# Cross-attention with token branch: another order for setup and the first two batches

## The chip, the cores and the metric

The kernel runs on one core of one Trainium2 chip. A core has five instruction queues that run beside each other: TensorE (PE, matrix products into PSUM; its weight loads are shown apart as PEld), VectorE (DVE), ScalarE (ACT), GpSimd (POOL, "Pool" below) and SyncE (SP), which here only issues DMA transfers. Each queue works in its own order; an instruction that waits holds up everything behind it on its queue. The metric is the device time of one execution in microseconds; the median of several executions is compared.

## What is computed

Sixteen batches of 100 queries and a context of 722 rows, of which the last four are "tokens". The parts that matter:

```python
query = hidden_states @ Wq;  keyt = enc @ Wk;  valt = enc @ Wv      # enc: 718 context rows x 384
hs = _mha(query, keyt, valt)                                        # 8 heads of 80
ca_q1 = jnp.einsum('btc,th->bch', ca, Wq_ca)[:, indices, :]         # ca: 4 tokens x 384
ca_hs1 = _mha(ca_q1, residual, residual)
ca_q2 = ca_hs1 @ Wq;  ca_k2 = ca @ Wk_ca;  ca_v2 = ca @ Wv_ca
ca_hs2 = _mha(ca_q2, ca_k2, ca_v2)
out = (hs + ca_hs2) @ Wout + b_out + residual
```

All of it is in 32-bit floats.

## The kernel before

**Context products with fewer multiplications.** The 718 context rows are cut into three thirds (240 columns each, u = 0, 1, 2), the 384 channels into three chunks, the 640 outputs into halves or pairs. From batch 1 on, a product of a batch's context with Wv (class `Values`, line 395) or Wk (class `Keys`, line 438) is made from 15 products of *forms* instead of 18: sums of the context's pieces times sums of the weights' pieces, listed in `V_PLAN` and `K_PLAN` with the PSUM bank, the form and the place that each feeds. The context's forms are made by `enc_sums` (line 466, 13 tensor_tensor of 128 x 240 on Pool for each batch; form 7 is the seventh written), the weights' forms once by `weight_sums` (line 487): seven early sums, which write fresh places, and five late ones, which overwrite raw weights, so everything that reads the raw weights must be done before them. Batch 0 uses raw pieces: `first_values` (line 353) and `first_keys` (line 561). The fifth block of 128 outputs of the keys is always made raw, by `last_keys` (line 568), whose two ScalarE copies into kT are line 554.

**Token branch.** Class `Second` does it per batch: `products` (y_ps and g), `scores1` (seven Pool instructions that form e from the tokens `ca` and g; lines 756 and 763), `softmax1` (its maximum by transposes on VectorE, lines 650 to 680, then line 773), `exponentials1`, `softmax2` (z_ps and z), `scores2` (lines 810 to 822), `softmax3` (lines 828 to 831), `load` (the tokens' values vb from DRAM, issued by Pool, line 802) and `values2` (seven Pool instructions into hs2, lines 845 and 852). `keys` (line 691) masks the small matrices m for a batch on Pool.

**One batch of the main loop** (from line 1089): `scores` (s_ps on PE, ScalarE copies to st, VectorE takes the row maximum `most`), `softmax2`, `products` of the next batch, `Maximum` of `most`, then the values of this batch and the keys of the next interleaved (`vv.go`, `kk.go`), `subtract` (line 1111) and `exponential` (line 1119) of three st tiles, `last_keys` of the next batch, now and then `project` (o_ps, which needs 128 finished rows; batches 0, 10 and 14 have none there), queries for the next two batches in odd batches, then the attention products a_ps (line 1272), which read st. hs, the result, has hs2 added (line 1294 in batch 0, line 1292 later) and is transposed by PE in the next batch (`Last.transpose`, line 891). Everything from line 1088 on is issued in the order in which it is written; above that a scheduler orders it, except the loads marked `in_order`.

**Setup.** SP loads the context of batch 0 (`load_first`), the tokens, Wq transposed (wqt, into wout_sb), x transposed (xT), Wk transposed in a packed order (wkt, into kT, five loads), Wq (five loads) and Wv of the tokens. PE makes the first values (v_ps), the token matrices (k_ps, m_ps, y_ps), turns wkt (w_ps, line 1028; copies alternately on ScalarE and VectorE, line 1031), then the first keys, va_ps and the queries. VectorE rearranges Wq into wq_sb (lines 1039 and 1046).

Buffers that matter: `rest` (one buffer, two context pieces of a batch), `enc` (two), `ca` (two), `hsT` (two), `vb` (one). The order in batches 0 and 1 around the change:

```python
if b == 0:                      # line 1128
    now.load()
    now.softmax1()
    for late in (False, True):
        weight_sums(nc.vector, wk_sb, late)
    enc_sums(enc)
    weight_sums(nc.gpsimd, wv_sb, False)
...
if b == 1:                      # line 1141, between the row maxima of tiles 1 and 2
    weight_sums(nc.vector, wv_sb, True)
```

Of the kernel before, what the change touches and what calls it, by code (L numbers as in the profile page):

```python
# [8 lines left out]
F32 = mybir.dt.float32  # L9
# [5 lines left out]
B, S, H = 16, 100, 640  # L15
NH, D = 8, 80
CAD, T = 384, 4
# [3 lines left out]
CC = CAD // P  # L21

KT = SK // 3 + 1
# [101 lines left out]
def kernel(  # L125
# [84 lines left out]
    def rest_tile(name):  # L210
        return main.tile([P, len(A_REST), KT], F32, tag="rest", name=name)
# [9 lines left out]
        return enc  # L221

    def load_rest(b, enc):
        rest = rest_tile(f"rest_{b}")
        for (u, c), i in A_REST.items():
            nc.sync.dma_start(
                out=rest[:, i], in_=enct[b][:, c, u * (KT - 1) : u * (KT - 1) + KT]
            )
        return enc[0], rest
# [9 lines left out]
    def in_order(dma):  # L239
        tc.keep_in_program_order(dma)  # L240
# [15 lines left out]
    def load_first(lo, hi, u, cols):  # L256

        for c in range(lo, hi):
            k = u * (KT - 1)
            in_order(  # L260
                nc.sync.dma_start(
                    out=a_raw(enc, u, c)[:, cols],
                    in_=enct[0][:, c, k + cols.start : k + cols.stop],
                )
            )
# [6 lines left out]
                in_=wv[c * P : (c + 1) * P, g * (H // 2) : (g + 1) * (H // 2)],  # L272
            )
    load_first(0, CC, 1, slice(KN, KT))
    for u in (2, 0):
        load_first(0, CC, u, slice(0, KT))
    tokens = vb_tile("tokens")
    cat_sb = tokens[:, CC, : CC * B * T].rearrange("p (c n) -> p c n", c=CC)
    wkca_sb = tokens[:, :CC, :]
# [2 lines left out]
    wqt_sb = wout_sb  # L282
    wkt_sb = kT.rearrange("p c u k -> p c (u k)")
    in_order(nc.sync.dma_start(out=wqt_sb, in_=wqt.rearrange("(c p) r -> p c r", p=P)))
    xT = inp.tile([P, 2, HC, S], F32, tag="xT", name="xT_0")
    in_order(nc.sync.dma_start(out=xT, in_=xt[0:2].rearrange("b p c s -> p b c s")))
    for c in range(HC):
        in_order(nc.sync.dma_start(out=wkt_sb[:, c, :CAD], in_=packed(wkt, c)))  # L288
    halves = [t[:, u] for t in [scores_tile(f"wq_{i}") for i in range(NP)] for u in range(2)]
# [83 lines left out]
    class Blocks:  # L373


        def __init__(self, plan):
            self.opened, self.begun = {}, set()
            self.plan = iter(enumerate(plan))
            self.ends = {bank: k for k, (bank, _, _) in enumerate(plan)}
# [181 lines left out]
    def first_keys(enc):  # L561
        for n in range(HC - 1):
            banks = [psum(f"kT_ps_0_{n}_{k}") for k in range(2)]
            weights = [wk_sb[:, 2 * c + n % 2, n // 2] for c in range(CC)]
            chunk_keys(n, banks, weights, enc)
        last_keys(0, enc)
# [136 lines left out]
    class Second:  # L703


        def __init__(self, b, xT):
            self.b, self.xT = b, xT[:, b % 2]
            self.top = None

            self.ca = small.tile([S, T, S], F32, tag="ca", name=f"ca_{b}", bufs=2)  # L710
            nc.sync.dma_start(
                out=self.ca, in_=cas[b].unsqueeze(0).to_broadcast([S, T, S])
            )
# [288 lines left out]
    for c in range(HC):  # L1002
# [12 lines left out]
            m_ps.rearrange("p (h b t) -> p h b t", h=NH, b=B),  # L1015
        )
        nc.sync.dma_start(out=m_d[c], in_=m_sb[c])
    second = Second(0, xT)
    keys(load_m(0))
    summed = second.products()  # L1020
    second.copy()
# [3 lines left out]
    for c in range(HC):  # L1025
        w_ps = psum(f"w_ps_{c}")
        for cc in range(CC):
            nc.tensor.transpose(
                w_ps[:, cc * P : (cc + 1) * P], wkt_sb[:, c, cc * P : (cc + 1) * P], ident
            )  # L1030
        (dve if c % 2 else act)(
            wk_sb[:, c % 2 : 6 : 2, c // 2] if c < HC - 1 else wk4,
            w_ps[:, : CC * P].rearrange("p (a n) -> p a n", a=CC),
        )

    with tc.issue_after(summed.ins):
        for c in range(HC):
            for u in range(2):
                nc.vector.tensor_copy(
                    wq_sb[:, c, 2 * u * P : 2 * (u + 1) * P].rearrange(  # L1040
                        "p (a r k) -> p a r k", a=2, r=RG
                    ),
                    wq_in[c].rearrange("p (r k) -> p r k", r=RG)[:, :, u * D : u * D + 64]
                    .rearrange("p r (a k) -> p a r k", a=2),
                )
            nc.vector.tensor_copy(
                wq_sb[:, c, 4 * P :].rearrange("p (h k) -> p h k", h=NH),
                wq_in[c].rearrange("p (h k) -> p h k", h=NH)[:, :, 64:],
            )
    first_keys(enc)  # L1050

    va = wide("va")[:, : H // 2]
    va_ps = psum("va_ps")
# [35 lines left out]
    for b in range(B):  # L1089
# [5 lines left out]
        def loads():  # L1095

            if b == 0:
                nc.sync.dma_start(
                    out=wout_sb, in_=wout.rearrange("(c p) n -> p c n", p=P)
                )  # L1100
            if b + 2 >= B:
                return None, None, None
            x_next = xT_at[0] if b % 2 else load_x(p + 1)
            xT_at[0] = x_next
            return Second(b + 2, x_next), load_enc(b + 2), load_m(b + 2)
# [12 lines left out]
        def exponential(i):  # L1118
            nc.scalar.activation(st[i], st[i], AF.Exp, scale=SCALE)  # L1119
# [6 lines left out]
            return most_now  # L1126

        if b == 0:
            now.load()
            now.softmax1()  # L1130
            for late in (False, True):
                weight_sums(nc.vector, wk_sb, late)
            enc_sums(enc)
            weight_sums(nc.gpsimd, wv_sb, False)
        st.append(scores(b, 0, tiles))
        if b == 0:
            now.exponentials1()
        nc.vector.tensor_tensor(most[:KN], st[0][:, 0], st[0][:, 1], ALU.max)
        st.append(scores(b, 1, tiles))
        larger(1)  # L1140
        if b == 1:
            weight_sums(nc.vector, wv_sb, True)
        st.append(scores(b, 2, tiles))

        now.softmax2()
# [6 lines left out]
            kk = Keys(b + 1, enc)  # L1152

        if b == 0:
            now.scores2()
            now.softmax3()
            second.scores1()
            top.go(3)
            kk.go(3)
            top.go(1)  # L1160
            first_values(3, e_in, (act, act), (0,), bank)
            kk.go(2)
            top.go()
            first_values(3, e_in, (act, act), (1,), bank)
            kk.go(3)
            first_values(0, e_in, (act, act), (0,), bank)
            kk.go(2)
            subtract(0)
            exponential(0)
            first_values(0, e_in, (act, act), (1,), bank)  # L1170
            kk.go(2)
            subtract(1)
            kk.go(3)
            exponential(1)
            second_next, enc_next, m_next = loads()
            last_keys(b + 1, enc)
            subtract(2)
            exponential(2)
            now.values2()
            second.load()  # L1180
            second.softmax1(4)
        elif b + 1 < B:
            last.transpose()
            vv = Values(b, e_in)

            def both(n):
                vv.go(n)
                kk.go(n)

            second.scores1(seen)  # L1190
            last.load()
            top.go(3)
            both(3)
            now.scores2()
            top.go(1)
            both(2)
            top.go()
            both(2)
            both(1)
            now.softmax3()  # L1200
            now.values2()
            vv.go(2)
            kk.go(1)
            subtract(0)
            exponential(0)
            vv.go(1)
            subtract(1)
            vv.go(1)
            kk.go(2)
            exponential(1)  # L1210
            vv.go(1)
            kk.go(2)
            both(1)
            both(1)
            second.load()
            second_next, enc_next, m_next = loads()
            subtract(2)
            last_keys(b + 1, enc)
            exponential(2)
            if b + 2 < B:  # L1220
                enc_next = load_rest(b + 2, enc_next)
            second.softmax1()
            last.project()
        else:
            room = enc_tile("spare").rearrange("p f k -> p (f k)")
            spare.extend(room[:, i * H : (i + 1) * H] for i in range(2))
            last.transpose()
            vv = Values(b, e_in)
            last.load()
            mine.load()  # L1230
            top.go(3)
            vv.go(3)
            last.project_few(len(OC) - 2)
            now.scores2()
            top.go(1)
            vv.go(2)
            top.go()
            vv.go(3)
            now.softmax3()
            now.values2()  # L1240
            vv.go(2)
            subtract(0)
            exponential(0)
            vv.go(5)
            for i in (1, 2):
                subtract(i)
                exponential(i)
            last.project()
        if b + 2 < B:
            if b == 0:  # L1250
                enc_next = load_rest(b + 2, enc_next)
            keys(m_next)
            enc_sums(enc_next)
        if b % 2 and b + 1 < B:
# [96 lines left out]
```

## Time and profile before

| What | Value |
|---|---|
| Executions shown | 961.81, 962.16, 964.65 us; median 962.16 |
| Profiled execution | 964.32 us, of which the span from first to last instruction is 962.6 us |
| Granted TensorE clock, mean | 0.995 |
| Busy: PE, PEld, DVE, ACT, POOL | 941.2 (98%), 799.9 (83%), 673.1 (70%), 359.1 (37%), 632.9 us (66%) |
| DMA | 62.48 MB, mean 65 GB/s |

The page cuts the span into 40 equal slices of 24 us, each digit being a busy share in tenths (9 is 90% or more):

```profile
PE   8898989999999999999999999999999999999998
DVE  1357796696947869496874959569694786928883
POOL 4269999485955768487673958738695576836613
PEclk9899999999999999999999999999999999999999
DMA  7930304022040301304050040401204031120100
```

PE is below nine tenths only in the first slices (setup and batches 0 and 1) and in the last. The chain that ended last is followed back from the last instruction to what released it:

```profile
PE 93%; DVE 2%; SPq 2%; DMA 2%; ACT 1%; issue 1%; ACTq 0%; DVEq 0%
```

A later batch takes about 56 us (a_ps starts at 165.6 us in batch 1 and at 902.8 us in batch 14); batch 0 begins near 67 us and batch 1 near 111 us of the span (the first scores, s_ps).

### The profile page before, as it was taken

Reading aid. Unit: us, or ns where it says so; the run is one execution under the profiler, and the core shown is the slowest. Engines: PE = TensorE matmul, PEld = TensorE weight load, DVE = VectorE, ACT = ScalarE, POOL = GpSimd, SP = SyncE. Lnnn points to the kernel's source line nnn. Section 1 sums busy time; section 2 is a strip of 40 time slices with the busy share of each in tenths; the row PEclk is TensorE's granted clock in tenths of the full one; section 3 lists DMA queues with packets and bytes.
Section 4 is the critical chain, followed back from the end, with each engine's and each line's share of the span. In section 5 each row is a group of like instructions: output and inputs, shape, how many; then the busy total and the mean of one; then the engine's idle time right before and its main releaser. Section 6 shows DMA issues by size and latency. Waiting matters only on the chain.

```text
span 962.6 us, 25608 instructions
## 1 busy us (share of the span) xinstructions
PE 941.2 (98%) x11215; PEld 799.9 (83%) x11215; DVE 673.1 (70%) x1083; ACT 359.1 (37%) x596; POOL 632.9 (66%) x572
## 2 busy tenths in 40 slices
PE   8898989999999999999999999999999999999998
PEld 6797869888798798978889787897879878898866
DVE  1357796696947869496874959569694786928883
ACT  1124433433424443342434334243432444325351
POOL 4269999485955768487673958738695576836613
PEclk9899999999999999999999999999999999999999
DMA  7930304022040301304050040401204031120100
GB/s 247 280 120 4 99 1 134 3 56 75 1 148 2 92 24 49 89 1 128 1 142 9 1 129 1 134 3 46 70 3 147 2 95 35 49 80 1 59 8 29
DMA packets 45256, 62.48 MB, mean 65 GB/s; under 512 B 13337, under 2 KB 37209, under 8 KB 43545
## 3 DMA queue, kind: packets, MB, share of 16 engines
q1 hardware_dynamic: 41608, 42.97, 15.1%
q0 software_dynamic: 2512, 16.72, 6.1%
q8 instruction: 88, 1.44, 0.6%
q10 hardware_dynamic: 1024, 1.15, 0.3%
q14 instruction: 24, 0.19, 0.1%
HBM read 55.26 MB, written 5.57 MB: 63 GB/s over the span
## 4 chain that ended last, share of the span: by engine, by line
PE 93%; DVE 2%; SPq 2%; DMA 2%; ACT 1%; issue 1%; ACTq 0%; DVEq 0%
PE s_ps L598 12%; PE a_ps L1272 11%; PE v_psA L419 10%; PE v_psB L419 8%; PE kT_ps L543 8%; PE k_psA L450 7%; PE q_ps L519 7%; PE o_ps L923 7%; PE k_psB L450 6%; PE v_psC L419 3%; PE k_psC L450 3%; PE v_psD L419 2%; PE v_psE L419 2%; PE y_ps L721 2%; PE k_psE L450 1%; SPq L288 1%
## 5 line engine op out<-in xcount | busy, mean ns | idle before, releaser
L756 POOL TENSOR_TENSOR e<-ca,g 100x800 f32<-100x800 f32 x64 | 99.3, 1562 | 155.4 <-DVE most L1123 118.7
L845 POOL TENSOR_TENSOR hs<-vb,p 100x640 f32<-100x640 f32 x64 | 105.6, 1660 | 42.5 <-DVE p L831 40.0
L1272 PEld LDWEIGHTS a_ps<-vs,st 120*64 120x64 f32 (+3 forms) x3072 | 109.1, 125 | 10.9 <-ACT st L1119 5.4
L852 POOL TENSOR_TENSOR hs<-hs,hs 100x640 f32<-100x640 f32 x48 | 115.3, 2402 | 3.8
L1272 PE MATMUL a_ps<-vs,st 120*64 120x81 f32 (+3 forms) x3072 | 112.5, 234 | 4.9 <-ACT st L1119 4.9
L419 PE MATMUL v_psA<-wv_sb,enc 128*120 128x320 f32 x360 | 113.2, 437 | 2.6 <-DVE wv_sb L506 2.6
L485 POOL TENSOR_TENSOR enc<-enc 128x240 f32<-128x240 f32 x135 | 103.9, 784 | 7.1
L1111 DVE TENSOR_TENSOR st<-st,over 120x1600 f32<-120x1600 f32 x48 | 108.0, 2253 | 0.0
L598 PE MATMUL s_ps<-qp,kT 32*120 32x100 f32 x3072 | 98.8, 263 | 0.7 <-issue 0.7
L598 PEld LDWEIGHTS s_ps<-qp,kT 32*120 32x120 f32 x3072 | 95.8, 179 | 2.5 <-issue 1.1
L763 POOL TENSOR_TENSOR e<-e,e 100x800 f32<-100x800 f32 x48 | 95.2, 1983 | 3.8
L615 ACT COPY st<-s_ps 120x800 f32<-120x800 f32 x64 | 49.7, 829 | 128.0 <-PE s_ps L598 128.0
L419 PE MATMUL v_psB<-wv_sb,enc 128*120 128x320 f32 x300 | 93.5, 434 | 0.0
L450 PE MATMUL k_psA<-enc,wk_sb 128*128 128x240 f32 x360 | 87.9, 367 | 2.5 <-DVE kT L390 1.4
L1283 DVE RECIPROCAL rs<-a_ps 100x4 f32<-100x4 f32 x32 | 5.8, 181 | 117.3 <-PE a_ps L1272 117.1
L419 PEld LDWEIGHTS v_psA<-wv_sb,enc 128*120 128x120 f32 x360 | 65.0, 184 | 26.0 <-issue 3.7
L450 PEld LDWEIGHTS k_psA<-enc,wk_sb 128*128 128x128 f32 x360 | 68.2, 190 | 19.9 <-DVE kT L390 1.9
L1123 DVE TENSOR_TENSOR most<-most,st 120x800 f32<-120x800 f32 x64 | 65.6, 1025 | 22.3 <-ACT st L609 21.2
L1119 ACT ACTIVATE st<-st 120x1600 f32<-120x1600 f32 x48 | 74.0, 1543 | 11.4 <-DVE st L1111 11.4
L419 PEld LDWEIGHTS v_psB<-wv_sb,enc 128*120 128x120 f32 x300 | 55.2, 184 | 22.5 <-issue 0.7
L450 PE MATMUL k_psB<-enc,wk_sb 128*128 128x240 f32 x300 | 73.0, 366 | 0.0
L485 POOL TENSOR_TENSOR enc<-enc,rest 128x240 f32<-128x240 f32 x45 | 34.7, 772 | 57.9 <-DMA rest<-in_enct 22.7
(138 smaller groups left out, 1762.5 us busy)
## 6 DMA issues: line engine op xcount, KB each, us to landing
vb<-va_d POOLq DMA_DIRECT2D x16, 1000.0 KB, 7.6
enc<-in_enct SPq DMA_DIRECT2D x30, 240.0 KB, 3.7
enc<-in_enct SPq DMA_DIRECT2D x15, 360.0 KB, 3.5
xT<-in_xt SPq DMA_DIRECT2D x8, 500.0 KB, 4.6
rest<-in_enct SPq DMA_DIRECT2D x31, 120.0 KB, 6.5
xn<-in_x SPq DMA_DIRECT2D x11, 320.0 KB, 9.2
out<-xn SPq DMA_DIRECT2D x11, 320.0 KB, 2.4
ca<-in_cas SPq DMA_DIRECT2D x16, 156.2 KB
```

The costliest lines, as they stand in the source:

```text
L419: nc.tensor.matmul(at[0][j][:KN, : H // 2], a_form(self.enc, f)[:, j * KN : (j + 1) * KN], wv_sb[:, W_AT[f]], start=first, stop=last, skip ...
L450: nc.tensor.matmul(at[:, i * KT : (i + 1) * KT], wk_sb[:, W_AT[f], i], a_form(self.enc, f), start=(first and i == 0), stop=last, skip_grou ...
L485: nc.gpsimd.tensor_tensor(out, left, right, op)
L543: nc.tensor.matmul(bank[:, i * KT : (i + 1) * KT], weights[c], a_raw(enc, u, c), start=(i == 0 and c == 0), stop=(c == CC - 1), skip_group ...
L598: nc.tensor.matmul(s_ps[r][:n, 256 * a + lo : 256 * a + hi], kT[rows, c, u, j * KN : (j + 1) * KN], rhs, start=(a == 0 and c == 0), stop=( ...
L756: first = nc.gpsimd.tensor_tensor(to, self.ca[:, t, :].unsqueeze(1).to_broadcast([S, NH, S]), g[:, :, t].unsqueeze(2).to_broadcast([S, NH, ...
L763: nc.gpsimd.tensor_tensor(e, e, to, ALU.add)
L845: first = nc.gpsimd.tensor_tensor(to, vb[:S, t, :].rearrange("p (h d) -> p h d", h=NH), p2[:, :, t].unsqueeze(2).to_broadcast([S, NH, D]), ...
L852: nc.gpsimd.tensor_tensor(sums, sums, to, ALU.add)
L1111: return nc.vector.tensor_tensor(st[i], st[i], top.over[:KN].unsqueeze(1).to_broadcast([KN, 2, ROWS]), ALU.subtract,)
L1119: nc.scalar.activation(st[i], st[i], AF.Exp, scale=SCALE)
L1272: nc.tensor.matmul(a_v[lo:hi, h % 4], st[i // 2][: KEYS[i], i % 2, h * S + lo : h * S + hi], block(i, h // 4)[: KEYS[i], h % 4], start=(i ...
```

## The change

Six things are moved; no instruction of the computation is added or left out; some change their engine.

- Weights' sums: the 12 of wk_sb and the seven early ones of wv_sb run on VectorE right after Wq has been rearranged, before the first softmax; the five late ones of wv_sb run on Pool at the end of batch 0 instead of VectorE in batch 1.
- Context's sums of batch 1 are issued on Pool ahead of the load of vb_0; those of batch 2 come after values2 of batch 0. vb_1 is loaded in batch 1, behind `scores1` of batch 2, instead of at the end of batch 0.
- In batch 0, `scores2` stands after the first keys and the maximum's first steps, `softmax3` after the keys' and values' additions; values2 waits for the last subtraction (`less`).
- In batches 0 to 14 the last exponential stands ahead of `last_keys` and so of its copies.
- Setup's loads: three context pieces go behind wqt; the tokens of batch 0 (`ca_0`) are loaded ahead of wkt; `rest_1` is loaded into a free hsT buffer.
- All five copies of w_ps run on ScalarE.

```diff
     def load_rest(b, enc):
-        rest = rest_tile(f"rest_{b}")
+        if b == 1:
+            room = hsT_tile("rest_1").rearrange("p c s -> p (c s)")
+            rest = room[:, : len(A_REST) * KT].rearrange("p (i k) -> p i k", k=KT)
+        else:
+            rest = rest_tile(f"rest_{b}")
...
-    for u in (2, 0):
-        load_first(0, CC, u, slice(0, KT))
+    load_first(0, CC, 2, slice(0, KT))
...
     in_order(nc.sync.dma_start(out=wqt_sb, in_=wqt.rearrange("(c p) r -> p c r", p=P)))
+    load_first(0, CC, 0, slice(0, KT))
     xT = inp.tile([P, 2, HC, S], F32, tag="xT", name="xT_0")
     in_order(nc.sync.dma_start(out=xT, in_=xt[0:2].rearrange("b p c s -> p b c s")))
+    ca_0 = small.tile([S, T, S], F32, tag="ca", name="ca_0", bufs=2)
+    in_order(nc.sync.dma_start(out=ca_0, in_=cas[0].unsqueeze(0).to_broadcast([S, T, S])))
...
-        (dve if c % 2 else act)(
+        act(
             wk_sb[:, c % 2 : 6 : 2, c // 2] if c < HC - 1 else wk4,
...
+    for w in wk_sb, wv_sb:
+        with tc.issue_after(summed.ins):
+            weight_sums(nc.vector, w, False)
     first_keys(enc)
+    weight_sums(nc.vector, wk_sb, True)
...
         if b == 0:
+            enc_sums(enc)
             now.load()
             now.softmax1()
-            for late in (False, True):
-                weight_sums(nc.vector, wk_sb, late)
-            enc_sums(enc)
-            weight_sums(nc.gpsimd, wv_sb, False)
...
-        if b == 1:
-            weight_sums(nc.vector, wv_sb, True)
...
         if b == 0:
+            second.scores1()
+            kk.go(3)
+            top.go(3)
             now.scores2()
-            now.softmax3()
-            second.scores1()
-            top.go(3)
-            kk.go(3)
             top.go(1)
...
             kk.go(3)
+            now.softmax3()
             first_values(0, e_in, (act, act), (0,), bank)
...
             second_next, enc_next, m_next = loads()
+            less = subtract(2)
+            exponential(2)
             last_keys(b + 1, enc)
-            subtract(2)
-            exponential(2)
-            now.values2()
-            second.load()
+            enc_next = load_rest(b + 2, enc_next)
+            keys(m_next)
+            weight_sums(nc.gpsimd, wv_sb, True)
+            now.values2(less)
+            enc_sums(enc_next)
             second.softmax1(4)
...
             second.scores1(seen)
+            if b == 1:
+                now.load()
             last.load()
...
             subtract(2)
+            exponential(2)
             last_keys(b + 1, enc)
-            exponential(2)
...
-        if b + 2 < B:
-            if b == 0:
-                enc_next = load_rest(b + 2, enc_next)
+        if 0 < b < B - 2:
             keys(m_next)
             enc_sums(enc_next)
```

`Second` takes the loaded `ca_0` as an argument for batch 0 instead of loading it itself.

## The prediction

> **What bounds the kernel now.** I read the share of busy time first: TensorE (PE) is busy 941.2 of 962.6 us and the chain that ended last is 93% PE, so time can be won only where PE stands still or runs at a lower clock. Next comes the list of who waited for whom, for PE alone:
>
> ```profile
> PE a_ps L1272 <- ACT st L1119: 4.9, 3, 1.6
> PE v_psA L419 <- DVE wv_sb L506: 2.6, 1, 2.6
> PE w_ps L1028 <- DMA kT<-in_wkt: 2.4, 1, 2.4
> PE m_ps L1005 <- DMA wout_sb<-in_wqt: 1.8, 1, 1.8
> PE k_psA L450 <- DVE kT L390: 1.4, 1, 1.4
> PE idle_ps L971 <- DVE idle L968: 1.1, 1, 1.1
> PE k_psA L450 <- ACT kT L392: 1.1, 1, 1.1
> PE s_ps L598 <- issue: 0.7, 1, 0.7
> PE kT_ps L543 <- DVE wk_sb L1031: 0.7, 1, 0.7
> ```
>
> Columns: total us, times, longest. All waits but two a_ps ones and the 0.7 of s_ps lie in the first 124 us. The timeline places them: a_ps at 104.79 (batch 0), 675.24 (batch 10) and 905.26 (batch 14), 1.64 us each; v_psA at 123.38 (batch 1); w_ps at 33.80; the k_psA waits at 82.01 and 86.94 (batch 0). The weight-load rows (PEld) of the same stalls read 1.80, 1.60 and 1.95 us; these are better, since ends of matmuls are modelled. Last, the windows around the wv_sb stall:
>
> ```profile
> 120.70:123.40 2.70, 0.07 (x2) 0.05 (x1) 2.67 (x4) 0.00 (x0) 2.62 (x4) 0.93 0.00 0
> 123.40:124.40 1.00, 1.00 (x2) 0.75 (x3) 1.00 (x2) 0.00 (x0) 0.92 (x2) 0.50 0.00 0
> 124.40:125.40 1.00, 1.00 (x3) 0.58 (x2) 0.97 (x3) 0.00 (x0) 1.00 (x2) 0.50 0.00 0
> 125.40:126.40 1.00, 1.00 (x3) 0.58 (x3) 1.00 (x3) 0.59 (x2) 1.00 (x2) 0.50 0.00 0
> 126.40:127.40 1.00, 1.00 (x5) 0.66 (x5) 0.96 (x2) 0.94 (x3) 0.92 (x2) 0.99 0.00 0
> ```
>
> After the length stand PE, PEld, DVE, ACT, POOL, then the granted clock: PE idles 2.7 us and then gets half the clock for 3 us.
>
> PE's own instructions stay the same (two m_ps products trade places), so each part is a question of which stall goes and what is late next.
>
> **Batch 1, weights' sums.** Five wv_sb sums (L506) sit on VectorE between the row maxima; v_psA waits for the third. From the first z_ps (118.40) to the first k_psA (128.18) batch 1 takes 9.78 us; batch 2, with the same order and no sums, takes 185.15 - 179.75 = 5.40. The stall's price is thus 4.38 us: 2.8 idle and some 1.6 of slow clock. [...] The row shows 0.50 after 2.7 us, so I take 4.4.
> The five sums move to Pool, behind the masked products of batch 2 and ahead of values2 of batch 0. Pool's row for this sum is 861 ns x7, so 4.3 us. What Pool then owes PE next is form 7 of batch 2's context for k_psA: the seventh of 13 sums (L485), which stand behind values2 in both orders. Before: values2 104.4 to 115.1, products to 119.0, seventh sum about 125.4, needed at 128.2. After: Pool's e products for batch 1 start when g is there (77.7, was 87.7) and are done by about 91; the mb load is issued when enc_0 is free (before: 96.3, some 2 us sooner now) and lands about 3 us later (longest wait 3.1); products to 100.5, sums to 104.8, values2 (9.7 alone: 4 x 1.27 + 3 x 1.55) to 114.5, seventh sum at 0.78 us a step about 120 to 121.5. PE, some 8 us ahead of before, asks at 120.4. I charge 0.5 us, with 0 and 2.5 as ends (2.5 if values2 is slowed as in its worst row, 2.79 for one product). hs2 at 114.5 holds up L1294 and the maxima behind it on VectorE, but the transposes of hs are not due before 116.5. **Gain 3.9.** If the Pool cover is gone, see rival 1.
>
> **Batch 0, VectorE and ScalarE order.** Three things leave VectorE: the 12 wk_sb sums (66.45 to 72.07), softmax3 ahead of the maximum, and the contention between the sums and Pool's enc_sums. The contention shows as one row: two Pool sums took 5.20 us at 65.74, where a free one takes 0.70. All 19 sums now run from about 39.4, where VectorE was idle 18.18 us until 57.60: by the row of nine in 3.09 us, 12 x 0.343 + 7 x 0.343 x 320/256 = 7.1 us, the last five not before first_keys is through with wk_sb (53.3), so to about 55. Pool's e products run there too, but with ca_0 there they start at about 31 instead of 45.43 and are done by about 44. The cover is that idle; without it 5.6 us would fall on softmax1. Pool's 13 sums then take some 10 us from 64, not 64.96 to 81.92, and seven wv sums (5.8 us) leave Pool.
> ScalarE: L822 no longer stands ahead of the three kT copies (81.28 behind a 3.19 us wait), so the first k_psA stall, 1.6, goes. The second then meets this row of the chain of waits:
>
> ```profile
> 79.98 0.52 DVE s L810
> ...
> 82.00 0.83 DVE p L831
> ...
> 85.88 0.32 DVE mx L662
> 86.22 0.67 DVE kT L390
> 86.94 1.08 PE k_psA L450 x4
> ```
>
> Without s, mx2, e, sm and p ahead (79.98 to 82.83) the transpose starts at 79.5 to 81, 3.45 us of maximum bring 83 to 84.5, scores2 now stands here (1.3), L390 ends at 85.0 to 86.4. PE could come at 83.4 (86.94 less the two stalls), so it waits 1.6 to 3.1 at this place, and the two stalls together shrink from 3.55 by 0.5 to 1.9; I take 1.4, near the better end because the maxima lose Pool's contention (2.54 and 2.38 for pairs whose free row is 0.99 each). VectorE's subtractions start as before (the copy that spreads the maximum ends near 86.4 to 87 and some 4 us of transpose, kT additions and softmax3 follow: 90.9 against 90.78), but run free of Pool's e products (1.82 each, were 1.82, 2.87, 2.03), so the last exponential can end near 101.7; PE comes to a_ps at 100.95 (102.37 less 1.4) and issues 0.65 us of products on the first two tiles. Stall left about 0.3 of 1.8: 1.5. **Gain 2.9**, ends 1.0 and 4.
>
> **Last exponential ahead of the kT copies, every batch.**
>
> ```profile
> 902.95 0.82 ACT L554 COPY kT<-kT_ps 128x480 f32<-128x480 f32 x2 [3.09 <-PE kT_ps L543]
> 903.65 1.55 ACT L1119 ACTIVATE st<-st 120x1600 f32<-120x1600 f32 x1
> ```
>
> ScalarE sat idle 3.09 us for the kT products while st was subtracted by 900.5 (L1111 at 897.99, 2.48 long). Swapped, the exponential ends at about 902.1, before a_ps starts at 902.84; the copies still follow their products, and kT is read only by the next scores. The stall goes in batches 10 and 14, the two with neither queries nor a projection between: 2 x 1.8, **gain 3.5** (ends 3.2 and 3.6). In the other batches (b=2: a_ps at 219.37, exponential done 216.35) nothing waited: nothing.
>
> **Setup.** On SP three enc loads of 120 KB go behind wqt, and ca_0 (156 KB) ahead of wkt. wqt comes about 1 us sooner, but PE then only waits longer at w_ps for wkt (33.77 before). Moved past ca_0, wkt is later. The row: in 22 to 24 us the DMA engines are busy 0.26 to 0.34 at 95 to 122 GB/s, so wkt moves on few engines; 156 KB at the 300 GB/s of the wide loads would be 0.5 us. [...] I take 0.6. The third wkt load must now also wait for wqt, with two of its kind still queued: nothing, up to one chunk's spacing (2.9 us) if they are gone. Against it, w_ps copies all on ScalarE free their banks at once, where VectorE's stood behind the wq copies (36.03): the weight-load wait of 1.06 goes. **Gain 0.5**, ends +1.5 and -2.3.
> The loads of rest_1 (into a free hsT buffer, early), rest_2 (behind mb) and vb_1 (issued by Pool behind the e products of batch 2, near 139, landing 7.6 later at 147, so values2 of batch 1 ends near 160; its first reader, L1292, comes at 161.5) cost nothing; that last cover is thin, but beyond it the hs transposes leave 10 us more.
>
> **Sum.** 3.9 + 2.9 + 3.5 + 0.5 = 10.8 us. The profiled execution took 964.32 (span 962.6 and 1.7 around it), so 953.5; the median of the runs shown is 962.16, 2.2 lower, so **951.3**.
>
> **Rivals.**
> 1. Pool is late in batch 1 and k_psA waits for form 7 as v_psA did for wv_sb, slow clock included. For it: 120.4 against 120 to 121.5; against: 13 sums after a free Pool. The 3.9 go: 955.2. Chance 0.14.
> 2. VectorE bounds batch 0: scores2 and the ScalarE copy behind L822 eat what softmax3 gave, the 2.9 go: 954.2. For it: L390 is still ahead of k_psA; against: 5.6 us of sums and the contention are gone. 0.15.
> 3. wkt is a chunk later, 2.9 us, and the half clock after it as long: 954.2. For it: the wait on wqt; against: two loads are queued. 0.10.
> 4. Slower. Only the swapped exponential repeats, so it alone could outweigh the rest. Where the last subtraction ends late, the exponential holds ScalarE and behind it the kT copies, their PSUM pair and the query copies, in 14 batches. At 1 us each it gives +14, 965.3; it decides from 0.8 us a batch. Against: in batch 2 the subtraction ends at 211.6, the exponential would by 213.2, and the copies cannot start before 214.1. 0.03.
>
> Main case 0.54; two rivals at once, down to no change, 0.04. Main case alone: 949 to 953.5. The range takes in rivals 1 to 3 and two of them half paid: 948 to 956.8. A measurement tells no change from about 0.3% (2.9 us): faster 0.93, same 0.04, slower 0.03.
>
> **What would show it.** No wait on wv_sb, z_ps to k_psA near 5.4 us in batch 1 and the clock at 1.0 there; a_ps without a wait in batches 10 and 14; one k_psA wait in batch 0, on L390; w_ps still waiting for wkt. Wrong: k_psA waiting for Pool's L485 near 120 us, w_ps waiting past 36, or a_ps waits in other batches.

## The result and the profile after

| | median (runs) | range | profiled span | mean clock |
|---|---|---|---|---|
| before | 964.08 us (11) | 961.81 to 966.66 | 962.6 us | 0.995 |
| after | 959.44 us (11) | 958.15 to 961.78 | 960.1 us | 0.992 |

The ratio is 0.996, 95% interval 0.9947 to 0.9973. Two executions further down, one of e8 (1337.45 us at a granted clock of 0.68) and one of before (2505.11 us at 1.00), were slow and are left out. The kernel became faster by 4.6 us in medians; 10.8 us were forecast, and 959.44 lies outside the range of 948 to 956.8. Before itself was 964.08 here, against the 962.16 on which the forecast was put, so 1.9 of the 8.1 us that the forecast missed by are its base and 6.2 are its sum. The list of who waited for whom begins for PE after the change with (total us, times, longest):

```profile
PE w_ps L1037 <- DMA kT<-in_wkt: 3.3, 1, 3.3
PE k_psA L456 <- POOL enc L491: 2.3, 1, 2.3
PE k_psA L456 <- DVE kT L396: 2.2, 1, 2.2
PE v_psD L425 <- DVE z L803: 1.6, 1, 1.6
PE s_ps L604 <- issue: 1.5, 1, 1.5
```

Every wait that the change aimed at is gone: a_ps on st, v_psA on wv_sb, k_psA on ScalarE. In their place stand three that before did not have or had shorter: k_psA on Pool's context sums, k_psA on the kT additions (2.2, was 1.4), v_psD on z. To see what each cost I took the starts of the same PE groups from both timelines and cut the span between them; the forecast for the same stretch stands last.

| stretch of PE | before, us | after, us | gain | forecast |
|---|---|---|---|---|
| start to first z_ps (setup, first scores) | 74.96 | 71.93 | +3.03 | 0.5 |
| z_ps to a_ps, batch 0 | 27.41 | 28.48 | -1.07 | 1.4 |
| a_ps of batch 0 to z_ps of batch 1 | 16.03 | 14.33 | +1.70 | 1.5 |
| z_ps to k_psA, batch 1 | 9.78 | 10.35 | -0.57 | 3.9 (with the next) |
| k_psA to a_ps, batch 1 | 37.39 | 39.06 | -1.67 | |
| a_ps of batch 1 to a_ps of batch 10 | 507.26 | 507.36 | -0.10 | 0 |
| a_ps of batch 10 to z_ps of batch 11 | 17.21 | 17.56 | -0.35 | 1.75 |
| to a_ps of batch 14 | 212.80 | 212.53 | +0.27 | 0 |
| a_ps of batch 14 to z_ps of batch 15 | 16.03 | 14.17 | +1.86 | 1.75 |
| to the end | 43.73 | 44.33 | -0.60 | 0 |

The gains add up to 2.50, which is 962.6 less 960.1. Batch 1 lost 2.24 where 3.9 were to be won. The timeline shows how, engine by engine (start, us, engine, line, operation; in brackets the idle time ahead and what ended it). PE:

```profile
118.73 1.24 PE L425 MATMUL v_psB<-wv_sb,enc 128*120 128x320 f32 x4
121.53 1.31 PE L425 MATMUL v_psD<-wv_sb,enc 128*120 128x320 f32 x4 [1.55 <-DVE z L803]
125.09 1.67 PE L456 MATMUL k_psA<-enc,wk_sb 128*128 128x240 f32 x4 [2.26 <-POOL enc L491]
126.56 1.81 PE L456 MATMUL k_psB<-enc,wk_sb 128*128 128x240 f32 x4
```

VectorE:

```profile
107.81 0.49 DVE L1296 TENSOR_TENSOR hs<-a_ps,rs 100x320 f32<-100x320 f32 x1
115.80 1.30 DVE L1305 TENSOR_TENSOR hs<-hs,hs 100x640 f32<-100x640 f32 x1 [7.50 <-POOL hs L861]
117.02 0.98 DVE L1148 TENSOR_TENSOR most<-st 120x800 f32<-120x800 f32 x1
118.10 2.70 DVE L1136 TENSOR_TENSOR most<-most,st 120x800 f32<-120x800 f32 x2
...
120.96 0.42 DVE L803 TENSOR_TENSOR z<-z_ps,rz 100x256 f32<-100x256 f32 x1
```

Pool:

```profile
86.28 1.89 POOL L772 TENSOR_TENSOR e<-e,e 100x800 f32<-100x800 f32 x1
98.25 2.46 POOL L702 TENSOR_TENSOR m<-mb,hmask 128x64 f32<-128x64 f32 x5 [10.08 <-DMA mb<-m_d]
100.67 4.29 POOL L512 TENSOR_TENSOR wv_sb<-wv_sb 128x320 f32<-128x320 f32 x5
104.92 3.28 POOL L854 TENSOR_TENSOR hs<-vb,p 100x640 f32<-100x640 f32 x2
...
115.72 0.69 POOL L491 TENSOR_TENSOR enc<-enc,rest 128x240 f32<-128x240 f32 x1
116.49 3.46 POOL L491 TENSOR_TENSOR enc<-enc 128x240 f32<-128x240 f32 x2
119.92 1.43 POOL L491 TENSOR_TENSOR enc<-rest,enc 128x240 f32<-128x240 f32 x1
121.43 3.61 POOL L491 TENSOR_TENSOR enc<-enc 128x240 f32<-128x240 f32 x3
```

Read from the bottom. k_psA needs the seventh context sum, which Pool ends at 125.04. The seven took 9.3 us, because VectorE's row maxima (L1136, L1148) and Pool's sums lie side by side from 115.7 on and both run long: a pair of sums takes 3.46, where the free ones behind them (from 125.00 on) take 0.69 each, and the two pairs of maxima take 2.70 and 2.38, where a pair in a later batch takes 2.0. They start only when values2 has ended, at 115.7; ahead of values2 stand the late sums of wv_sb, ahead of these the masked products, and ahead of those Pool is idle for 10 us, waiting for the mask. On VectorE the same lateness of values2 holds L1305; behind it in the queue stand three maxima and then z, which frees the bank that v_psD needs. PE thus stops twice, for 1.55 and 2.26 us, and then has half clock from 125.42 to 128.84.

What the mask hangs on is shown by the chain of waits (start, us, what):

```profile
90.91 1.63 PE v_ps L366 x6
92.54 0.02 issue
92.56 0.57 SPq L217
...
94.39 3.72 DMA mb<-m_d
98.11 0.02 issue
98.14 0.02 POOLq L702
```

The mask is queued on SP behind the context loads of batch 2, and these need the buffer that PE's last first values of batch 0 read until 92.5. So the masked products, the late sums, values2 and the context sums all move with PE's batch 0.

Batch 0 lost 1.07 ahead of a_ps. The windows there (length; busy PE, PEld, DVE, ACT, POOL; granted clock; DMA share; GB/s):

```profile
83.30:84.30 1.00, 1.00 (x5) 0.95 (x6) 0.66 (x1) 0.99 (x2) 1.00 (x1) 1.00 0.03 8
84.30:85.30 1.00, 1.00 (x5) 0.87 (x4) 0.46 (x1) 0.98 (x3) 0.92 (x2) 0.58 0.00 0
85.30:86.30 1.00, 1.00 (x4) 0.86 (x3) 1.00 (x2) 0.29 (x1) 0.92 (x2) 0.50 0.00 0
86.30:87.30 1.00, 1.00 (x4) 0.81 (x3) 0.75 (x2) 0.00 (x0) 1.00 (x1) 0.50 0.00 0
```

PE came back at 83.29 after 2.17 us of waiting for the kT additions, ran one us at full clock, and then 3.4 at half (84.47 to 87.88). Before, the two shorter stops here (1.1 and 1.4 us) had no such tail.

### The profile page after: what moved, and what is told of

Read it like the earlier page. It is cut to its first block, busy times and chain, and to the rows that moved or that the text cites. A ratio compares the mean times of both kernels' runs of the same rounds, so it can differ in the third digit from the quotient of the medians.

```text
span 960.1 us, 25609 instructions
## 1 busy us (share of the span) xinstructions
PE 942.0 (98%) x11215; PEld 801.9 (84%) x11215; DVE 674.0 (70%) x1083; ACT 361.8 (38%) x598; POOL 620.1 (65%) x570
## 4 chain that ended last, share of the span: by engine, by line
PE 91%; DMA 3%; POOL 2%; DVE 1%; issue 1%; SPq 0%; ACT 0%; ACTq 0%; DVEq 0%; POOLq 0%
PE s_ps L604 11%; PE a_ps L1283 11%; PE v_psA L425 10%; PE v_psB L425 8%; PE k_psA L456 7%; PE kT_ps L549 7%; PE q_ps L525 7%; PE o_ps L932 7%; PE k_psB L456 6%; PE v_psC L425 3%; PE k_psC L456 2%; PE v_psE L425 2%; PE v_psD L425 2%; PE y_ps L730 2%; PE k_psE L456 1%; DMA wout_sb<-in_wqt 1%
## 5 line engine op out<-in xcount | busy, mean ns | idle before, releaser
L491 POOL TENSOR_TENSOR enc<-enc 128x240 f32<-128x240 f32 x135 | 101.1, 763 | 7.1
L772 POOL TENSOR_TENSOR e<-e,e 100x800 f32<-100x800 f32 x48 | 90.5, 1886 | 3.8
L1294 DVE RECIPROCAL rs<-a_ps 100x4 f32<-100x4 f32 x32 | 5.8, 181 | 114.9 <-PE a_ps L1283 114.9
L1136 DVE TENSOR_TENSOR most<-most,st 120x800 f32<-120x800 f32 x64 | 66.0, 1031 | 22.4 <-ACT st L615 21.2
L491 POOL TENSOR_TENSOR enc<-enc,rest 128x240 f32<-128x240 f32 x45 | 31.8, 706 | 74.2 <-DMA rest<-in_enct 27.4
```

The costliest lines, as they stand in the source:

```text
L491: nc.gpsimd.tensor_tensor(out, left, right, op)
L772: nc.gpsimd.tensor_tensor(e, e, to, ALU.add)
```

## The experiments

Times are medians; "before" is the kernel before, run beside each. Theory and rival stand in each expectation.

| run | time, us (runs) | before beside it | ratio, 95% interval |
|---|---|---|---|
| e1_exp_only | 961.0 (22) | 963.59 | 0.9975, 0.9967 to 0.9982 |
| e2_setup_only | 963.18 (13) | 963.59 | 0.9989, 0.9976 to 1.0002 |
| e3_sums_first | 955.12 (5) | 963.59 | 0.9915, 0.9902 to 0.9928 |
| e4_both | 954.68 (5) | 963.59 | 0.9906, 0.9893 to 0.992 |
| e5_copies_only | 962.97 (21) | 964.19 | 0.9991, 0.9983 to 0.9998 |
| e6_loads_only | 964.48 (14) | 964.19 | 1.0002, 0.9991 to 1.0013 |
| e7_batch0_order | 957.75 (6) | 964.19 | 0.9933, 0.9919 to 0.9948 |
| e8_subtract_early | 954.58 (3) | 964.19 | 0.9897, 0.9882 to 0.9911 |
| e9_sums_vector | 952.91 (4) | 964.95 | 0.9875, 0.9862 to 0.9889 |
| e10_exp_14 | 960.89 (5) | 964.95 | 0.9963, 0.9949 to 0.9976 |
| e11_exp_10 | 963.27 (15) | 964.95 | 0.9983, 0.9974 to 0.9992 |

**Batch 1: Pool's order (e3).** The changed kernel with two lines of batch 0 exchanged, so that the late sums fill Pool's wait for the mask:

```diff
             enc_next = load_rest(b + 2, enc_next)
-            keys(m_next)
             weight_sums(nc.gpsimd, wv_sb, True)
+            keys(m_next)
             now.values2(less)
```

> The changed kernel with one edit: on Pool the five late wv_sb sums stand ahead of the masked products of batch 2, where Pool idles 10 us for the mb load. Theory A (position on Pool): values2 of batch 0 starts 4.3 us earlier (100.7 instead of 104.9), hs2 is done near 111.5, the two waits of batch 1 (v_psD on VectorE's z, k_psA on Pool's sum) and the half clock after them go, z_ps to k_psA in batch 1 falls from 10.35 to about 5.4 us, and the time is 6 to 7 us below the changed kernel, near 953. Theory B (contention of Pool's context sums with VectorE's row maxima): both still run side by side from 112 on, the seventh sum stays late, k_psA waits 1.5 us or more, and the gain is under 3 us.

Pool's timeline of this kernel:

```profile
89.99 5.86 POOL L512 TENSOR_TENSOR wv_sb<-wv_sb 128x320 f32<-128x320 f32 x5 [3.38 <-PE v_ps L366]
96.76 2.48 POOL L702 TENSOR_TENSOR m<-mb,hmask 128x64 f32<-128x64 f32 x5 [0.92 <-DMA mb<-m_d]
99.20 2.50 POOL L854 TENSOR_TENSOR hs<-vb,p 100x640 f32<-100x640 f32 x2
...
114.93 4.36 POOL L491 TENSOR_TENSOR enc<-enc 128x240 f32<-128x240 f32 x3
```

and PE's:

```profile
119.34 1.08 PE L456 MATMUL k_psA<-enc,wk_sb 128*128 128x240 f32 x4 [0.50 <-POOL enc L491]
120.26 0.97 PE L456 MATMUL k_psB<-enc,wk_sb 128*128 128x240 f32 x4
```

The late sums now lie in the 10 us in which Pool stood idle, the mask is still what comes last, and values2 starts at 99.2 instead of 104.9. The wait of v_psD is gone, that of k_psA is 0.5, the clock stays up (k_psB 0.97, was 1.81), and z_ps to k_psA takes 6.06 us. The context sums still contend with the maxima (4.36 for three): their contention costs little once they start five us earlier. The time is 4.3 us below that of the changed kernel, between the figures of the two theories (6 to 7, and under 3); in the profiles batch 1 is 5.5 us shorter from z_ps to a_ps (43.88 against 49.41). Pool's place of five instructions was the main fault of the change.

**Batch 0: what stands ahead of the kT additions (e7, e4).** In the changed kernel the last pair of row maxima runs beside Pool's products of batch 1 (3.22 us for the pair), and both it and `scores2` stand ahead of the kT addition on which k_psA waits. The edit, alone in e7 and together with the exchange above in e4:

```diff
-            second.scores1()
+            second.scores1(seen)
             kk.go(3)
             top.go(3)
-            now.scores2()
             top.go(1)
             first_values(3, e_in, (act, act), (0,), bank)
             kk.go(2)
+            now.scores2()
             top.go()
```

(`seen` makes Pool's products of batch 1 wait for the last maximum, so that they do not contend with it; the pair took 2.01 us in e7.)

> The edit of the run before plus, in batch 0, scores2 behind the kT additions and Pool's e products of batch 1 held until the row maximum is through. Theory A: the k_psA wait in batch 0 (2.2 us and 1.7 us of half clock behind it) goes as well, since the first kT addition ends near 80.6 us, when TensorE comes; time 3.5 us below the run before, near 950. Theory B: the wait moves to the next thing that VectorE or ScalarE owes (the second a_ps tile, softmax3), TensorE reaches a_ps at the same time as in the run before, and the gain over it is under 1 us.

> The changed kernel with batch 0's edit alone (maxima of softmax2 behind the kT additions of the first three groups); Pool keeps the masked products ahead of the late sums, so batch 1 keeps its waits. Theory A (a wait given back later: what batch 0 wins is waited again for Pool's seventh sum of batch 1, since nothing of Pool's chain moves): wait on kT of 2.2 us gone and clock 1.00 in 84 to 88, but the k_psA wait on enc in batch 1 grows from 2.3 to 3.5 to 5 us, time within 0.7 us of the changed kernel's 959.4. Theory B (the half clock of batch 0 is worth its 1.7 whatever follows): 957.0 to 958.0.

In e7's windows the stop and the half clock behind it are gone:

```profile
83.00:84.00 1.00, 1.00 (x7) 0.94 (x5) 0.96 (x2) 0.15 (x1) 1.00 (x1) 1.00 0.00 0
84.00:85.00 1.00, 1.00 (x6) 0.80 (x5) 1.00 (x2) 0.54 (x2) 0.92 (x2) 1.00 0.00 0
85.00:86.00 1.00, 1.00 (x5) 0.68 (x4) 0.90 (x3) 0.00 (x0) 1.00 (x1) 1.00 0.00 0
```

z_ps to a_ps takes 24.83 us, 3.65 less than in the changed kernel. My theory A for e7 was that batch 1 would wait longer for Pool by as much; it did not. The waits of batch 1 are 1.6 and 2.3 as in the changed kernel, and Pool's row says why:

```profile
95.74 2.32 POOL L702 TENSOR_TENSOR m<-mb,hmask 128x64 f32<-128x64 f32 x5 [4.41 <-DMA mb<-m_d]
```

The mask came 2.5 us sooner (95.74, was 98.25), because it hangs on PE's first values; the chain of Pool moved along with PE. In time e7 is 1.7 us below the changed kernel, theory B's figure, though the two ratios' intervals touch (0.9919 to 0.9948 against 0.9947 to 0.9973). Part of the 3.65 went back behind batch 1's waits, where the half clock lasted from 120.81 to 127.64, twice as long as in the changed kernel: k_psA to a_ps takes 39.91, not 39.06. In e4, with Pool's sums ahead of the mask, the same edit brought only 0.4 us on top of e3, theory B's figure. z_ps to a_ps falls from 28.49 to 24.98, but a_ps of batch 0 then waits 1.9 us for the last exponential, and the stretch behind it grows from 14.41 to 16.25: the subtractions lie beside Pool's sums and take 3.37 and 2.18 us where a free one takes 1.82. That is the contention moved, not removed. It accounts for 1.8 of the 3.5 us; the two profiles differ by 1.6, each being of the fastest execution of its kernel, and five executions each do not tell 0.4 from 1.6.

**Following that wait (e8, e9).** e8 is e4 with the second subtraction ahead of two kT additions; e9 is e8 with the five late sums on VectorE:

```diff
+            subtract(1)
             kk.go(2)
-            subtract(1)
             kk.go(3)
             exponential(1)
...
-            weight_sums(nc.gpsimd, wv_sb, True)
+            weight_sums(nc.vector, wv_sb, True)     # e9 only, behind the last subtraction
             keys(m_next)
```

> The version with both repairs, and the second subtraction of batch 0 ahead of two kT additions. Theory A (the a_ps wait of 1.9 us comes from VectorE's 1.2 us idle ahead of the two kT additions, with the subtractions contending with Pool's sums behind it): the subtraction starts near 87.7 instead of 90.2, the last exponential ends near 96.5 to 97, the a_ps wait of batch 0 falls to below 0.6, and the time to 953.0 to 953.9. Theory B (the kT additions come late instead, and k_ps banks are waited for): the a_ps wait is replaced by one of 0.5 to 1.5 us on kT, time within 0.6 us of 954.7.

> The version with both repairs and the early subtraction, and the five late sums of wv_sb on VectorE behind the last subtraction of batch 0 (1.7 us at 0.34 each) instead of on Pool (4.3 to 5.8 us). Theory A (Pool's chain of products, sums, keys and values2 alone sets the seventh sum of batch 1): values2 starts about 2.9 us sooner, near 96.6, the k_psA wait on Pool of 2.1 us goes, and the time is 952.0 to 953.0. Theory B (the seventh sum is late because Pool's sums and VectorE's maxima contend, wherever they start, or because the mask load lands late): a k_psA wait above 1.2 us stays and the time lies within 0.6 us of 954.6.

In e8 the a_ps wait on the exponential is gone, as theory A said, and the time is the same as e4's, as theory B said; of theory B's wait on kT there is 0.6 us. Where the rest of the gain went stands on Pool and PE:

```profile
87.24 5.18 POOL L772 TENSOR_TENSOR e<-e,e 100x800 f32<-100x800 f32 x1
...
119.51 1.08 PE L456 MATMUL k_psA<-enc,wk_sb 128*128 128x240 f32 x4 [2.08 <-POOL enc L491]
```

The subtraction that came earlier now lies beside Pool's last product of e, which took 5.18 us where a free one takes 1.88; everything behind it on Pool is later, and k_psA waits 2.1 us for the seventh sum. e9 takes 4.3 to 5.8 us off Pool for

```profile
96.01 2.69 DVE L512 TENSOR_TENSOR wv_sb<-wv_sb 128x320 f32<-128x320 f32 x5
```

on VectorE. The k_psA wait falls to 0.8 and the time to 952.91 us, inside theory A's band, though values2 starts at 98.3 and not 96.6: the products' mask is again last (Pool idle 2.53 for it). This is the lowest median: 1.25% below before (1.11 to 1.38%) and 6.5 us below the changed kernel's 959.44. The interval overlaps that of e8, so the 1.7 us between those two are not certain.

**The last exponential (e1, e10, e11).** The kernel before with the exponential ahead of the copies in all batches but the last; in batch 14 alone; in batch 10 alone (the cut of the later batches; in batch 0 of e1 the subtraction goes ahead of the copies too):

```diff
             subtract(2)
-            last_keys(b + 1, enc)
             exponential(2)
+            last_keys(b + 1, enc)
```

> The kernel before with one edit: the last exponential ahead of the last keys' copies in batches 0 to 14. Theory A (the prediction's step): the three a_ps waits go, the product rows of a_ps show no wait on st, and the time falls by 3 x 1.8 = 5.4 us. Theory B: only those waits go, but batch 0 is bound by VectorE's subtractions just behind, so batch 0 keeps about 1 us of its wait and the gain is 3.5 to 4.5 us. Theory C (the slower rival): the copies, held behind the exponential, cost time in the other batches, and the gain is under 2 us or a loss.

> The kernel before with the last exponential ahead of the kT copies in batch 14 alone. Theory A (each a_ps wait is worth its 1.8 us unless something behind it takes it back; in batch 10 the wait for issue at the next scores takes part): the a_ps wait of batch 14 goes, those of 0 and 10 stay, and the time falls by 1.4 to 2.4 us, nearly all of what the swap in all batches gave (2.4). Theory B (both batches are worth the same): 1.0 to 1.3 us.

> The same swap in batch 10 alone. Theory A: the a_ps wait of batch 10 goes, the wait for issue of s_ps behind it grows from 0.7 to 1.3 to 1.7 us, with up to 4 us of half clock, and the time falls by 0 to 0.8 us. Theory B: 1.0 to 1.8 us less, and the wait for issue stays at 0.7.

The waits of a_ps in batches 10 and 14 go wherever the swap is made; batch 0 keeps 1.2 us in e1. Theory C's cost in the other batches is not there: a_ps of batch 1 to a_ps of batch 10 takes 507.22 in e1 and 507.26 before. In batch 14 the stretch from a_ps to the next z_ps falls from 16.03 to 14.18 in e1 and e10, all of the 1.85. In batch 10 it falls from 17.21 to 15.91 and 15.92 (e1, e11): 1.3, since a wait that no engine explains ("issue") grows behind it from 0.74 to 1.40 (e1's row):

```profile
682.33 0.78 PE L598 MATMUL s_ps<-qp,kT 32*120 32x100 f32 x20 [1.40 <-issue]
```

In the five profiles without this swap the stretch takes 16.55 to 17.80 (mean 17.15), in the eight with it 15.45 to 17.56 (mean 16.07), so about 1.1 is the surer figure.

The two together are thus worth some 3 us in the profiles. The times say 2.4 (e1, below theory B's 3.5), 1.7 (e11) and, for batch 14 alone, 0.37%, or 3.6 us (2.3 to 4.9): e10's gain is over both theories' bands and over what its edit did in the profile; its profile also has a shorter setup with the setup's code unchanged (below), and all five of its executions were short (960.05 to 962.14), which chance in one execution does not explain. I take the 1.85 of the stretch and leave the rest open. e11's 1.7 us leans to theory B, its issue wait of 1.4 to theory A; batch 10 keeps most of its gain.

**The setup (e2, e5, e6).** The kernel before with the loads' order, `ca_0` and the copies (e2); with the copies alone (e5); with the loads alone (e6). The core of the copies' edit:

```diff
-        (dve if c % 2 else act)(
+        act(
             wk_sb[:, c % 2 : 6 : 2, c // 2] if c < HC - 1 else wk4,
```

> The kernel before with the setup's part alone: three context loads behind wqt, the tokens of batch 0 ahead of wkt, all five w_ps copies on ScalarE. The prediction gave this 0.5 us. Theory A (from the changed kernel's trace): the keys' products then follow the turned weights without a gap, TensorE's half clock ends some 3.5 us earlier, and the first z_ps starts about 3 us earlier, near 72.0 instead of 74.96 us; time down by 2.5 to 3 us. Theory B: the 3 us came from the weights' sums leaving VectorE, or were chance of the clock; then the first z_ps stays at 74 to 75 us and the time moves by under 1 us.

> The kernel before with one line changed: all copies of w_ps go to ScalarE. Theory A (the gap of 0.66 us ahead of the first context product is what keeps the clock at half): the context products follow w_ps without a gap, at about 35.9, the half clock ends near 37 to 38 instead of 41, and the first z_ps stands at 72.8 to 73.6 (before 74.96, with the whole setup edit 71.97); by time some 1 us at most, since part is given back at the wv_sb stall. Theory B (the loads' order sets it): first z_ps within 0.7 of 74.96.

> The kernel before with only the loads changed: the three enc loads behind wqt, the mask of batch 0 ahead of wkt; VectorE keeps half of the w_ps copies. Theory A: w_ps goes on 0.6 us earlier (33.2 against 33.8), the gap ahead of the context products and the half clock to about 41 stay, first z_ps at 74.2 to 74.6. Theory B: the half clock ends before 38 and the first z_ps is near 72. The prediction's term (the mask makes wkt 0.6 later) would have w_ps go on at 34.4.

The first z_ps comes at 71.97 in e2, at 71.82 in e5 (earlier than either of its theories said) and at 75.16 in e6 (later than its theory A); in the changed kernel it came at 71.93, so nothing there points to the weights' sums, which e2 leaves where they were. In e6 w_ps goes on at 32.78 instead of 33.80, but the keys still start at 36.43, behind a copy on VectorE (a wait of 1.86), and the half clock lasts to about 41.6: what the loads bring, that copy gives back. In e5 half clock ends at 36.6. By time the copies give 0.9 us by the ratio (0.2 to 1.6), the loads nothing, and the two together in e2 0.4 us in medians, not told from none (a gain of 2.3 to a loss of 0.2); of the 3.1 us that e5 leads by at the first z_ps, 1.3 have gone by a_ps of batch 1 (lead 1.8), where v_psA still waits for wv_sb. In e2 3.0 shrink to 1.7 in the same way.

But a profile holds one execution, and the setup varies from one to the next. e10's setup is that of before, yet there w_ps began later, at 31.84 (29.73 before), and no longer had to wait for the last wkt load:

```profile
32.87 2.01 PE L1028 MATMUL w_ps<-ident,kT 128*128 128x128 f32 x13
```

Its first z_ps stands at 72.10; in the four profiles with the old setup it stands at 72.10, 73.90, 74.96 and 75.47 (mean 74.1), in the seven with the new one at 70.38 to 72.94 (mean 71.9). The new setup is thus worth about 2.2 us at that point, not 3.0, and in the old order it is not all kept. The place of the first z_ps goes with the number of 3.41 us steps that the granted clock spent at half before it: none in e3 (70.38); one in e10, e5 and five with the new setup (70.86 to 72.76); two in before, e1, e11, e6 and, with the new setup, e7 (72.94 to 75.47).

## Why the forecast was wrong

**Batch 1, weights' sums: "Gain 3.9".** This is the step that failed. Its price for the wv_sb stall was right: with the sums out of the way and Pool early enough, e3 has z_ps to k_psA in 6.06 us, against 5.9 by the forecast (5.40 and 0.5). Its end times for Pool's first two steps were right too, to 0.2 us (products to 100.5, measured 100.7; late sums to 104.8, measured 104.96), but by luck: the setup's unforeseen 2.5 us and the 2.5 us missing in batch 0 (1.4 forecast, 1.07 lost) cancelled, so that PE reached a_ps of batch 0 at 100.41, against 100.95 in the forecast. Wrong were two terms behind them. values2 took 10.8 us, not "9.7 alone" (it had taken 10.7 before, by the forecast's own "104.4 to 115.1"); and the seventh sum came at 125.0, not 120 to 121.5, since "0.78 us a step" became 1.33 for seven sums beside VectorE's maxima. In before the same seven, beside one pair of maxima and the five weights' sums, took 6.6 us (119.00 to 125.58); a free step of Pool was the wrong row for this place. And the sentence that hs2 "holds up L1294 and the maxima behind it", harmless because the transposes come late, stopped following the queue one instruction too soon: behind the maxima stands z, and v_psD waits for z. With the half clock behind, the step lost 2.24 us. Rival 1 named the wait but priced it as the loss of the gain only, with nothing below zero.

**Batch 0, VectorE and ScalarE: "Gain 2.9".** The first k_psA stop went, as forecast, and the last exponential no longer holds a_ps (1.70 gained, 1.5 forecast). The second stop was forecast at 1.6 to 3.1 and was 2.17. But I priced it as idle time alone, while pricing the wv_sb stall one paragraph earlier with its half clock. The tail cost about 1.7 us in batch 0; the net is 0.63 us. e7 shows the same place without the stop and without the tail. Rival 2 named the cause (scores2 ahead of L390). Rivals 1 and 2 together give 958.1 (951.3, 3.9 and 2.9), near the 959.44 that came, but the parts do not fit: batch 1 missed by 6.1 and not 3.9, and the setup's 2.5 us made up for it. All pairs of rivals had 0.04, and the range ended at 956.8.

**Last exponential: "gain 3.5".** Right in its mechanism: both waits went, with no wait in any other batch. Batch 14 gave 1.86. Batch 10 gave 1.3 in e1 and e11 against before; in the changed kernel's profile it gave nothing, because there the issue wait of 1.5 us was followed by half clock:

```profile
682.40:683.40 1.00, 1.00 (x24) 1.00 (x24) 0.00 (x0) 0.00 (x0) 1.00 (x2) 0.50 0.00 0
683.40:684.40 1.00, 1.00 (x28) 1.00 (x25) 0.00 (x0) 0.73 (x2) 0.92 (x3) 0.50 0.00 0
```

**Setup: "Gain 0.5".** Mis-sized, about 2.2 at the first z_ps. The forecast counted the wait of 1.06 us for the copies and not that the half clock can end a step of 3.41 us sooner (36.58 in e5, 41.09 before); whether it does varied between executions. By time the setup alone (e2) gained 0.4 us, so there the 0.5 is not contradicted. The feared 0.6 us for wkt behind ca_0 did not show: w_ps went on at 33.16 (33.80 before) and at 32.78 in e6. The 0.6 us was my estimate, and no run here shows such a cost. Rival 3 (wkt a chunk late) did not happen.

**The clock.** Taking the half clock from the row (0.50 behind 2.7 us without work) was right: the changed kernel shows it behind shorter stops too, of 2.17 us in batch 0 and 2.26 in batch 1. The traces have a step of 3.41 us (last section), and PE need not stand still for the whole of one: it was busy for 0.34 of the step ahead of the half clock in batch 1 of before and for 0.37 of the one in batch 0 of the changed kernel. The forecast used the row for one stop only.

In sum: 10.8, less 6.1 for batch 1, 2.3 for batch 0 and 2.0 for the exponential, plus 2.5 for the setup, less 0.4 elsewhere, gives the 2.5 us between the two profiles. The medians are kinder (4.6). The remaining 0.6 us in the stretch to the end is in this one profile only; no other run with that code has it (43.78 to 43.98), and I leave it open.

## What to carry to other kernels

Work taken off a critical engine should go where its new engine waits for a load, not behind that wait: moving five instructions ahead of the mask's products was worth 4.3 us. When something is late, follow its queue to the end, past the instructions that are harmless, until one is found that frees a buffer of the bounding engine; and take durations from rows with the same neighbours, since instructions of VectorE and Pool took up to 3.7 times longer side by side here (a pair of Pool's sums 5.20 us before, at 65.74, where a free one takes 0.70). A stop of the bounding engine should be priced twice, as its length alone and with the half-clock tail that some such stops had here (about 1.7 us in batch 0). Parts of this change were never run alone: the early weights' sums on VectorE, and the loads of `rest_1` and vb_1.

## What the runs showed of the hardware

- The half clock is not decided by the length of a stop alone: a stop of 2.08 us in e8 had none behind it, one of 1.49 us in batch 10 of the changed kernel had. In all 13 traces the granted clock changes only on a grid of 3.41 us, which lies differently in each execution, and every half-clock stretch but the one at the end is one or two steps long: 34.26 to 41.09 and 123.01 to 126.42 in before (26 steps between the two starts), and 33.27 to 36.68, 84.47 to 87.88, 125.42 to 128.84 and 681.80 to 685.22 in the changed kernel. In these traces the half clock goes mostly with how much of one step PE stood still. Between 60 and 935 us, of the full-clock steps in which PE was busy for 0.40 or less, all 10 were followed by half clock; of those with 0.42 to 0.56, 2 of 18 (1.49 us of stop in batch 10 of the changed kernel, at 0.56, and batch 1 of e11, at 0.43); of those with more, none. The ends of PE's instructions are modelled, so the borders are rough, and what decides between 0.42 and 0.56 is open. Two steps of before, around the stop of 2.7 us in batch 1 (busy us out of 3.41, then the clock):

```profile
119.59:123.00 3.41, 1.17 (x13) 0.98 (x11) 3.41 (x4) 0.52 (x1) 3.25 (x5) 1.00 0.09 29
123.01:126.42 3.41, 3.04 (x6) 1.97 (x7) 3.34 (x7) 0.61 (x2) 3.33 (x4) 0.50 0.00 0
```

  and two of e8, whose stop of 2.08 us had no tail:

```profile
115.99:119.40 3.41, 1.45 (x6) 0.67 (x4) 3.31 (x4) 2.69 (x6) 3.33 (x3) 1.00 0.00 0
119.41:122.82 3.41, 3.31 (x15) 2.93 (x16) 3.21 (x10) 1.68 (x3) 3.25 (x6) 1.00 0.00 0
```

- The wait for issue in batch 10 (0.2 to 1.8 us in the runs' profiles, within the first s_ps after a_ps of that batch) has no engine behind it. In the changed kernel the DMA engines were 0.90 to 1.00 busy from 673 to 678 us, 0.10 in the us of the stop (679 to 680), and packets of the instruction queue lie between 677 and 678 and between 681 and 682; before, they were 0.81 to 1.01 busy from 675 to 680, and the stop came only at 682.2. What made PE's next instructions late was not shown.
- One Pool product of 100 x 800 beside VectorE's subtractions took 5.18 us, where it takes 1.88 free; a pair of context sums took 3.46, where two free ones take 1.38.
